# One-hots of the edge index from ScalarE to VectorE, and S1·T1 of row pairs in seven products of quarters, in a relational graph layer

## The chip, the cores and the metric

The kernel runs on one core of one Trainium2 chip. The metric is device time in microseconds (us) of one execution. The text calls the engines as the profile does: PE (TensorE, matmuls), PEld (its weight loads), DVE (VectorE), ACT (ScalarE), POOL (GpSimd), SP (SyncE, which issues DMAs).

## What is computed

1250 nodes have 1024 features each; 20,000 edges have a source, a target and one of 8 types. After a layer norm and a relu, h is multiplied with eight weight matrices of 1024 x 1024; every node takes, per type, the mean of its incoming neighbours' products, plus h times a root matrix; a gate with tanh mixes the result with h. In short:

```python
h = maximum(layernorm(x), 0)
u = h @ root + bias
for r in range(8):
    mask = edge_type == r
    sums = segment_sum(h[src] * mask, dst)
    cnt = segment_sum(mask, dst)
    u = u + (sums / maximum(cnt, 1)) @ weight[r]
z = concatenate([u, h]) @ w_gate + b_gate
out = x + tanh(u) * z + h * (1 - z)
```

All values are f32. The edges' sources, targets and types are inputs, so the order of the edges must be worked out on the chip.

## The kernel before

**Matrices and products.** The kernel multiplies h with each of the eight weights first and gathers rows of the products afterwards. There are eleven matrices in `mats`: the eight weights (numbers s = 0 to 7), the root, and two halves of the gate matrix. The text counts them from one: matrix two is s = 1. h stands in ten blocks of 128 rows, and product i (0 to 4) of a matrix takes blocks i and i + 5. Of these two blocks and the matrix it makes a 2 x 2 arrangement, A11, A12, A21, A22 times B11, B12, B21, B22, each B a quarter of 512 x 512, and forms the result by seven products in place of eight: A11·B11, A12·B21, S4·B22, A22·T4, S1·T1, S2·T2, S3·T3, where S and T are sums of A and B quarters (`left`, L406, and `make_t1` to `make_t4`, L172 to L186, on DVE). Every one of the seven is four f32 matmuls of 128x512 (`add`, L428, rows L430). The function `product` (L414) writes them out in a fixed order: p1 (A11), p5 (S1, L485), S2, p7 (S3), p3 (S4), A22. Results go from PSUM to a row tile by copies on ACT and by adds on DVE.

**Pairs.** In matrices two to ten, products 0 and 1, and 2 and 3, make a pair (`paired`, L571). The first of a pair is the head; the fifth product, number 4, stands alone (`lone`). Two products of a pair have the same B quarter in each of the seven, so such a quarter can again be cut 2 x 2, into pieces of 256 x 256, and formed by seven products of quarters, each two matmuls of 128x256 (`Second.add`, L219, rows L221). Class `Second` (L188) does this for A12·B21, class `First` (L323) for A11·B11 in all paired matrices, class `Third` (L261) for S4·B22 from matrix five on. `First` runs half of its work ahead, at the end of the product before (`early`, L343), and the rest in the head (`late`, L354): its two results lie in two PSUM banks, `to0` for the head and `to1` for the second product. Its sums are in a small room of SBUF tiles (`room`); `sums` and `next_sums` (L274, L280: two rows of 128x256 and two of 128x512 each) fill it twice. S1·T1 is done whole in both products of a pair, 4 matmuls in each (p5).

**PSUM.** There are eight banks: four named ps (`bank`, L122), two named ps_b (`lead`), one ps_n, one ps_q.

**Steps.** After each part, `done` (L434) calls `between` with a running number. `beside` (L618) hangs the matrix sums and weight loads on these numbers, and then one step of whatever else is to be done beside the products. From the first matrix to the fourth that is `norms_and_index` (L1368): a generator that goes one piece further at every step, except at the (product, step) places listed at L1385. `fill` places the quarter products between the parts.

**The index.** `slots` (L1080) goes over the edges in rounds of four chunks of 128. Each round takes two steps. In the first, `one_hots` (L1095) writes `is_lo` (which of 128 low key values an edge has, four tiles of 128x128 in bf16) by |a - b| (four ACT rows, L1100) and relu(1 - x) (one ACT row, L1102), and `is_at` on DVE (L1105). In the second, PE looks up and counts (`look` L1165, `count` L1111, bf16 matmuls), DVE takes the counts (`pick`, `add_counts`, `residue`), `place` (L1182) finds each edge's rank by four rows at L1190, and `to_los` (L1157) writes the other one-hot, 128x512, by two ACT rows (L1161, L1162). Counts of a round use the one-hots of the round before; the lookup of a round uses sums from the round before it. Every four rounds `to_table` (L1196) works out the places of up to 16 chunks, and `scatter` (L1067) issues two indirect DMAs of POOL at each step (rows L1071). `order` (L1220) and `rows_and_weights` (L809) follow; the rows are gathered (`add_slot`, L1422) beside matrices six and later.

**Queues.** Each engine works in program order. SP and ACT issue weight loads and plain stores, POOL the indirect DMAs.

Of the kernel before, what the change touches and what calls it, by code (L numbers as in the profile page):

```python
# [21 lines left out]
def tile_rgcn_highway(  # L22
# [31 lines left out]
    nc = tc.nc  # L54
# [28 lines left out]
    LATE = 4  # L83
    IDLE = 12
# [36 lines left out]

    def bank():  # L122
        return psum.tile([P, 512], F32, name="ps", bufs=4)

# [136 lines left out]
    class Third:  # L261
# [24 lines left out]
        def hold(self):  # L286
            self.c0 = psum.tile([P, CG, P], F32, name="ps_n", bufs=1).rearrange("p c k -> p (c k)")
            return self.c0
# [76 lines left out]

    def transposed(aop, part, of, n, relu=False):
# [47 lines left out]
    def product(aop, w, to, between=lambda j: None, last=None, pieces=1, whole=True,  # L414
                fill=None, second=None, third=None, inner=None, first=None, early=None, own=(),
                aside=None, head=False, lone=False):
# [21 lines left out]
        def filled(name):  # L438
            if fill and name in fill and fill[name]():
                done()  # L440

# [9 lines left out]
        def p7():  # L451
            d = c21 if third is None else aside()
            add(b, S3)
            nc.scalar.copy(d, b)  # L454
            nc.vector.tensor_add(c22, c if lone else c22, d)  # L455
            done()
            filled("seventh")
            return d
# [16 lines left out]
        def p1():  # L475
            if first is None:
                b = lead()
                add(b, A11, True)
            else:
                b = first.late() if head else first.to1  # L480
            nc.scalar.copy(c11, b)  # L481
            done()
# [3 lines left out]
        def p5(c=None):  # L486
            if c is None:
                c = inner.hold() if inner and inner.holds else held("ps_n")
# [9 lines left out]
        if first and head and early is None and "first" not in fill:  # L498
            c = inner.hold() if inner else bank()
# [15 lines left out]
        filled("sixth")  # L515
# [67 lines left out]
    waiting, waiting_third, waiting_first = {}, {}, {}  # L583
# [10 lines left out]
    def step(s, i, between=lambda j: None, second=None):  # L594

        two = paired(s, i)
        if (s, i) == (NM - 2, NP - 1):
# [5 lines left out]
        if two and i % 2 == 0:  # L603
            waiting[i] = Second(fac[s], i), t[0]

# [12 lines left out]
        def beside(j):  # L618
# [6 lines left out]
            if two and i % 2 == 0 and j == 3:  # L625
                waiting_first[s, i].fifth_to()
# [14 lines left out]
            if (s, i, j) == (0, 0, 3) or (s > 0 and (i, j) == (3, int(thirds(s)))):  # L641
# [27 lines left out]
        coming = next_first(s, i)  # L669

# [10 lines left out]
        if two:  # L681
# [18 lines left out]
            elif i == 1:  # L700
# [7 lines left out]
                else:  # L708
                    fill.update(seventh=lambda: (e.fourth(), e.to_second(t[0]),
                                                 put(i - 1, 0, to), 0)[-1],  # L710
                                third=lambda: (e.fourth_to_second(t[0]), 0)[-1])
            elif i == 2 and q:
# [9 lines left out]
            elif q:  # L722
                fill = dict(first=lambda: (q.first(t[1][:, :Q]), e.fourth(), e.to_second(t[0]),
# [4 lines left out]
            else:  # L728
                fill = dict(first=lambda: (e.to_second(t[0]), e.fourth_to_second(t[0]), 0)[-1],
# [4 lines left out]
                head=i % 2 == 0, lone=i == NP - 1,  # L734
# [9 lines left out]

    for _ in range(IDLE):
        nc.tensor.matmul(bank()[:, :P], ident, ident, start=True, stop=True)
    eps = const.tile([P, 1], F32, name="eps")
# [88 lines left out]
    with ExitStack() as early:  # L836
# [151 lines left out]
        less_lo = ix1.tile([P, NCH], F32, name="less_lo")  # L988
# [5 lines left out]
        less_pid = ix1.tile([P, 1], F32, name="less_pid")  # L994
# [6 lines left out]
        def columns():  # L1001
# [49 lines left out]
            nc.vector.tensor_single_scalar(less_lo, part_i, -1.0, op=OP.mult)  # L1051
# [8 lines left out]
            nc.vector.tensor_single_scalar(less_pid, pid, -1.0, op=OP.mult)  # L1060
# [6 lines left out]
        def scatter(count):  # L1067

            for c in placed[:count]:
                n = nedges(c)  # L1070
                ins = nc.gpsimd.indirect_dma_start(  # L1071
                    out=table[:, :],
                    out_offset=bass.IndirectOffsetOnAxis(ap=at_i[:n, c:c + 1], axis=0),
                    in_=row_col[:n, c:c + 1], in_offset=None,
                    bounds_check=G * KEYS * SLOTS - 1, oob_is_err=False)
                tc.declare_no_dep(ins.ins, query=no_wait, group="scatter", reason="each edge has its own slot")
                tc.add_to_no_dep_group("scatter", ins.ins)
            del placed[:count]

        def slots(ix):  # L1080
# [14 lines left out]
            def one_hots(j):  # L1095
# [3 lines left out]
                for i in range(m):  # L1099
                    nc.scalar.activation(is_lo[:, i, :], io, AF.Abs,  # L1100
                                         bias=less_lo[:, c0 + i:c0 + i + 1])
                nc.scalar.activation(is_lo[:, :m, :], is_lo[:, :m, :], AF.Relu, scale=-1.0,  # L1102
                                     bias=1.0)
# [53 lines left out]
            def to_los(j):  # L1157
# [3 lines left out]
                nc.scalar.activation(to_lo[:, :m, :], o["l_bc"][:, :m, :], AF.Abs, bias=less_pid)  # L1161
                nc.scalar.activation(to_lo[:, :m, :], to_lo[:, :m, :], AF.Relu, scale=-1.0,  # L1162
                                     bias=1.0)
# [32 lines left out]
            def to_table(c0, c1):  # L1196
# [3 lines left out]
                over = ix.tile([P, AT * CG], F32, name="over", bufs=1)  # L1200
                nc.vector.tensor_single_scalar(over[:, :m], rank[:, at], float(SLOTS), op=OP.is_ge)
                where = ix.tile([P, AT * CG], F32, name="where", bufs=1)
                nc.vector.tensor_add(where[:, :m], first[:, at], rank[:, at])
                nc.vector.scalar_tensor_tensor(at_i[:, at], over[:, :m], float(FAR), where[:, :m],  # L1204
                                               op0=OP.mult, op1=OP.add)
                placed.extend(range(c0, c1))

            load_keys(0)
            for j in range(ng + 3):
                for f, of in ((one_hots, j), (load_keys, j + 1), (as_bf16, j - 2),  # L1210
# [3 lines left out]
                    if f is None:  # L1214
                        scatter(CG // 2)
# [4 lines left out]
        def order():  # L1220

            with tc.tile_pool(name="sort", bufs=1) as sp:
# [12 lines left out]
                for _ in range(7):  # L1235
# [661 lines left out]
```

## Time and profile before

| what | value |
|---|---|
| median of 3 runs | 1334.18 us (1333.55 to 1334.95) |
| the profiled execution's own time | 1332.95 us |
| its span, first to last instruction | 1331.2 us |
| granted TensorE clock, mean | 0.998 |
| busy PE / DVE / ACT / POOL | 1318.1 / 957.4 / 386.8 / 573.4 us |
| L1100, L1102 on ACT | 157 rows, 50.1 us; 40 rows, 0.39 to 0.63 us each |
| L1161, L1162 on ACT (to_lo) | 39 rows of 128x512 each, 28.1 and 24.6 us |
| L1190 on DVE | 157 rows, 55.0 us, each with a read of its accumulator of 0.08 us |
| first and last start of L1071 (scatters) | 123.1 and 414.2 us |

A row of the profile groups instructions of one line, engine, operation and tile names: "out<-in" with their partitions and elements, how many, busy time together and the mean of one. Busy times of one engine count overlapping rows once. The views used below are the page, the waits, the timeline (instructions in order of time) and stretches (busy time of each engine in given windows).

### The profile page before, as it was taken

To read this page: it belongs to the slowest core of one execution; us is meant where nothing else is said; L and a number is where in the kernel's file an instruction comes from. 1 tells how busy PE (TensorE), PEld (TensorE's weight loads), DVE (VectorE), ACT (ScalarE), POOL (GpSimd) and SP (SyncE) were. 2 spreads that over 40 slices of the span, in tenths; PEclk is the share of its full clock that TensorE was granted. 3 is DMA by queue.
4 is the path that set the end of the run, shared out by engine and by line. 5 is a ranking of instruction groups with operands and counts; after the bars stand their busy time and mean duration, and the time that the engine had idled before them with its cause. 6 is when DMAs were issued, how large, how long until landed. Compare 5 with 4: busy or idle time off the path is not lost.

```text
span 1331.2 us, 13340 instructions
## 1 busy us (share of the span) xinstructions
PE 1318.1 (99%) x4120; PEld 716.5 (54%) x4120; DVE 957.4 (72%) x1825; ACT 386.8 (29%) x800; POOL 573.4 (43%) x510
## 2 busy tenths in 40 slices
PE   9999999999999999999999999999999999999997
PEld 5444555555455545655655565565565556644443
DVE  7757755665674664458987988897788799857875
ACT  3476556464621111211121211122121112221210
POOL 0002663744553156202353546446255556615631
PEclk9999999999999999999999999999999999999999
DMA  8877346642734251143748779877778957969961
GB/s 315 295 222 198 63 92 139 139 77 69 185 75 96 87 114 47 52 158 122 251 127 315 240 249 351 280 245 270 264 265 317 350 184 244 318 247 295 343 166 60
DMA packets 116799, 263.72 MB, mean 198 GB/s; under 512 B 33150, under 2 KB 44818, under 8 KB 116592
## 3 DMA queue, kind: packets, MB, share of 16 engines
q1 hardware_dynamic: 56528, 112.62, 28.1%
q0 software_dynamic: 44064, 118.20, 28.0%
q10 hardware_dynamic: 16128, 31.98, 7.8%
q8 instruction: 33, 0.54, 0.2%
q14 instruction: 46, 0.38, 0.1%
HBM read 202.34 MB, written 75.41 MB: 209 GB/s over the span
## 4 chain that ended last, share of the span: by engine, by line
PE 91%; issue 3%; DMA 2%; DVE 2%; POOL 1%; SPq 1%; ACT 0%; POOLq 0%; DVEq 0%
PE ps_b L430 44%; PE ps L430 18%; PE ps L221 14%; PE ps_n L430 5%; PE ps_b L221 4%; PE ps_q L221 2%; PE ps_q L430 2%; PE ps_n L221 2%; DMA xt<-in_x_dram 1%; DMA w<-in_L_gnn_weight_dram 1%; DMA h_op<-in_L_gnn_b_gate_dram 0%; POOL out_dram L770 0%; SPq L850 0%; PE ps L373 0%; PE ps_q L1114 0%
## 5 line engine op out<-in xcount | busy, mean ns | idle before, releaser
L430 PE MATMUL ps_b<-w,h_op 128*128 128x512 f32 x1464 | 659.7, 595 | 1.0 <-ACT row L513 0.8
L430 PEld LDWEIGHTS ps_b<-w,h_op 128*128 128x128 f32 x1464 | 273.6, 190 | 308.1 <-issue 296.4
L1425 POOL DMA_INDIRECT got<-y,idx x193 | 247.6, 1283 | 289.8 <-DVE u L1430 183.3
L1430 DVE SCALAR_TENSOR_TENSOR u<-got,w_of,u 128x1024 f32<-128x1024 f32 (+1 forms) x193 | 247.0, 1282 | 36.3 <-DMA got<-y,idx 33.2
L430 PE MATMUL ps<-w,h_op 128*128 128x512 f32 (+1 forms) x592 | 264.9, 589 | 0.3 <-ACT row L493 0.3
L1071 POOL DMA_INDIRECT table<-row_col,at_i x157 | 168.6, 1074 | 135.4 <-DVE at_i L1204 52.1
L430 PEld LDWEIGHTS ps<-w,h_op 128*128 128x128 f32 x592 | 111.0, 190 | 121.4 <-issue 115.0
L454 ACT COPY row<-ps_b 128x512 f32<-128x512 f32 x53 | 31.1, 586 | 188.0 <-PE ps_b L430 188.0
L455 DVE TENSOR_TENSOR row<-row 128x512 f32<-128x512 f32 x44 | 30.3, 689 | 75.2 <-ACT row L454 75.2
L430 PE MATMUL ps_n<-w,h_op 128*128 128x512 f32 x176 | 80.1, 592 | 0.0
L513 ACT COPY row<-ps_b 128x512 f32<-128x512 f32 x54 | 31.6, 586 | 162.1 <-PE ps_b L430 162.1
L221 PE MATMUL ps<-w,h_op 128*128 128x256 f32 x288 | 74.4, 381 | 0.0
L221 PE MATMUL ps<-w,w 128*128 128x256 f32 x288 | 71.1, 380 | 0.0
L553 ACT COPY row<-ps_b 128x512 f32<-128x512 f32 x40 | 23.4, 585 | 161.1 <-PE ps_b L430 140.8
L221 PEld LDWEIGHTS ps<-w,h_op 128*128 128x128 f32 x288 | 54.1, 190 | 27.6 <-issue 21.6
L221 PE MATMUL ps<-inner 128*128 128x256 f32 x264 | 67.8, 379 | 0.0
L221 PEld LDWEIGHTS ps<-w,w 128*128 128x128 f32 x288 | 54.6, 190 | 21.8 <-issue 15.8
L1190 DVE SCALAR_TENSOR_TENSOR junk<-k_bc,key_col,before 128x128 f32<-128x128 int16 x157 | 55.0, 350 | 4.2
L221 PEld LDWEIGHTS ps<-inner 128*128 128x128 f32 x264 | 50.1, 190 | 14.6 <-issue 8.4
L430 PEld LDWEIGHTS ps_n<-w,h_op 128*128 128x128 f32 x176 | 33.4, 190 | 39.5 <-issue 39.2
L481 ACT COPY row<-ps_b 128x512 f32<-128x512 f32 x54 | 31.6, 586 | 73.3 <-PE ps_b L430 68.7
L1100 ACT ACTIVATE is_lo<-io,less_lo 128x128 bf16<-128x128 f32 x157 | 50.1, 391 | 0.0
(246 smaller groups left out, 1473.7 us busy)
## 6 DMA issues: line engine op xcount, KB each, us to landing
y<-row SPq DMA_DIRECT2D x72, 512.0 KB
w<-in_L_gnn_weight_dram ACTq DMA_DIRECT2D x21, 1024.0 KB
w<-in_L_gnn_weight_dram SPq DMA_DIRECT2D x10, 1024.0 KB
w<-in_L_gnn_w_gate_dram ACTq DMA_DIRECT2D x6, 1024.0 KB
k_bc<-keys_dram SPq DMA_DIRECT2D x39, 128.0 KB
l_bc<-los_dram SPq DMA_DIRECT2D x39, 128.0 KB
h_dram<-h_op SPq DMA_DIRECT2D x9, 512.0 KB
u<-in_L_gnn_bias_dram SPq DMA_DIRECT2D x9, 512.0 KB
```

Of the source, the lines that this page charges most:

```text
L221: nc.tensor.matmul(p, a[:, k, :], b[:, k, :], start=(fresh and k == 0), stop=(k == 1), skip_group_check=True)
L430: nc.tensor.matmul(b[:, at], aop[:, i, k, :], w.of[i][:, k, at], start=(fresh and k == 0), stop=(k == KQ - 1), skip_group_check=True)
L454: nc.scalar.copy(d, b)
L455: nc.vector.tensor_add(c22, c if lone else c22, d)
L481: nc.scalar.copy(c11, b)
L513: nc.scalar.copy(c12, b)
L553: nc.scalar.copy(c21, b)
L1071: ins = nc.gpsimd.indirect_dma_start(out=table[:, :], out_offset=bass.IndirectOffsetOnAxis(ap=at_i[:n, c:c + 1], axis=0), in_=row_col[:n, ...
L1100: nc.scalar.activation(is_lo[:, i, :], io, AF.Abs, bias=less_lo[:, c0 + i:c0 + i + 1])
L1190: nc.vector.scalar_tensor_tensor(junk, o["k_bc"][:, i, :], key_col[:, c:c + 1], before, op0=OP.is_equal, op1=OP.mult, accum_out=rank[:, c: ...
L1425: nc.gpsimd.indirect_dma_start(out=t[:n], out_offset=None, in_=y[g][:, :], in_offset=bass.IndirectOffsetOnAxis(ap=at[:n, d, k:k + 1], axis=0),
L1430: nc.vector.scalar_tensor_tensor(u[:n], t[:n], w, u[:n], op0=OP.mult, op1=OP.add)
```

## The change

There are two parts, and some that go with them.

S1·T1 of the pairs of matrices two to five (`FIFTHS`, s from 1 to 4) is formed by a new class `Fifth`, seven products of quarters. Its first result lies in bank ps_n, its second in a kept bank of the four ps, set up once by a matmul on the identity. In the head it begins before A11, adds a quarter after it, does two after S2 and three after S3; the second product has no S1·T1 matmuls of its own. A step with the number 9 (`TICK`) is added after S3 of a head, and one after S2 of product 2; two places, (1, 1) and (3, 1), join the list at L1385. The quarter products of A12 move to other places of products 2 and 3. The lone product of these matrices uses the kept bank for S1·T1. Of the 12 matmuls on the identity at the start, four become one of 512 columns.

The one-hots `is_lo` and `to_lo` are written by DVE in one compare each: `is_lo` from a bf16 copy of the counting row against a column of low key values, `to_lo` from the int16 keys against the partition's number. The positions of a round are made at the start of the next steps, four chunks at a time, and the round's four scatters are issued there.

```diff
+    def sum_bank(odd):
+        if odd:
+            if not kept:
+                kept.append(bank())
+                nc.tensor.matmul(kept[0].rearrange("p (c k) -> p c k", c=CG), ident,
+                                 ident[:, None, :].to_broadcast([P, CG, P]), start=True, stop=True)
+            return kept[0]
+        return psum.tile([P, CG, P], F32, name="ps_n", bufs=1).rearrange("p c k -> p (c k)")
...
+    class Fifth:
...
+        def begin(self):
+            self.to0 = sum_bank(0)
+            self.x = bank()[:, :H]
+            Second.add(self, self.x, self.a11, self.b11, True)
+            nc.scalar.copy(self.to0[:, :H], self.x)
+        def second(self):
+            Second.add(self, self.to0[:, :H], self.a12, self.b21)
+        def early(self):
+            y = bank()[:, :H]
+            Second.add(self, y, self.s1, self.t1, True)
+            nc.scalar.copy(self.p5, y)
+            Second.add(self, self.x, self.s2, self.t2)
+            nc.vector.tensor_add(self.to0[:, H:], self.x, self.p5)
+        def late(self):
+            self.to1 = sum_bank(1)
+            Second.add(self, self.x, self.s1, self.t1)
+            nc.scalar.copy(self.to1.rearrange("p (a n) -> p a n", a=2),
+                           self.x[:, None, :].to_broadcast([P, 2, H]))
+            Second.add(self, self.to0[:, H:], self.s2, self.b22)
+            Second.add(self, self.to1[:, :H], self.a22, self.t2)
+        def fifth_to(self):
+            nc.vector.tensor_add(self.to1[:, H:], self.to1[:, H:], self.p5)
...
     def p7():
             add(b, S3)
             nc.scalar.copy(d, b)
+            if root and head:
+                between(TICK)
+                root.late()
+                nc.scalar.copy(c22, c)
+                root.fifth_to()
...
     def p1():
                 b = first.late() if head else first.to1
+            if root and head:
+                root.sums()
+                first.fifth_to()
             nc.scalar.copy(c11, b)
+            if root and head:
+                root.second()
...
     def p5(c=None):
+            if root:
+                c = root.to1
...
+        if root and head:
+            root.begin()
+            c = root.to0
+            if inner:
+                inner.c0 = c
+            b = p1()
...
         nc.scalar.copy(c12, b)
         done()
-        filled("sixth")
+        if root and head:
+            root.early()
+            root.next_sums()
+        if not filled("sixth") and root and head:
+            done()
...
                 for i in range(m):
-                    nc.scalar.activation(is_lo[:, i, :], io, AF.Abs,
-                                         bias=less_lo[:, c0 + i:c0 + i + 1])
-                nc.scalar.activation(is_lo[:, :m, :], is_lo[:, :m, :], AF.Relu, scale=-1.0,
-                                     bias=1.0)
+                    nc.vector.tensor_scalar(is_lo[:, i, :], io_b, lo_col[:, c0 + i:c0 + i + 1],
+                                            None, op0=OP.is_equal)
...
-                nc.scalar.activation(to_lo[:, :m, :], o["l_bc"][:, :m, :], AF.Abs, bias=less_pid)
-                nc.scalar.activation(to_lo[:, :m, :], to_lo[:, :m, :], AF.Relu, scale=-1.0,
-                                     bias=1.0)
+                nc.vector.tensor_scalar(to_lo[:, :m, :], o["l_bc"][:, :m, :], pid, None,
+                                        op0=OP.is_equal)
...
-                if s > 0 and (i, j) in ((0, 0), (1, 5), (NP - 1, 4)):
+                if s > 0 and (i, j) in ((0, 0), (1, 1), (1, 5), (3, 1), (NP - 1, 4)):
```

## The prediction

> **What bounds the kernel now.** I read four views, from the whole to the place. First the page: its head, its busy times, the row PE and the granted clock in the 40 slices, and the chain that ended last.
>
> ```profile
> span 1331.2 us, 13340 instructions
> ...
> PE 1318.1 (99%) x4120; PEld 716.5 (54%) x4120; DVE 957.4 (72%) x1825; ACT 386.8 (29%) x800; POOL 573.4 (43%) x510
> ...
> PE   9999999999999999999999999999999999999997
> ...
> PEclk9999999999999999999999999999999999999999
> ...
> PE 91%; issue 3%; DMA 2%; DVE 2%; POOL 1%; SPq 1%; ACT 0%; POOLq 0%; DVEq 0%
> ```
>
> PE has work 99% of the span, at full clock, and the chain runs through it for 91%. So a matmul that is taken out shortens the run by its own length, as long as no new wait stands in its place. The waits of PE say how little other engines hold it up today: the longest that belongs to the products is one of 0.6 us.
>
> ```profile
> PE ps_b L430 <- ACT row L513: 0.8, 1, 0.8
> ...
> PE ps_b L221 <- ACT ps_b L347: 0.6, 1, 0.6
> ```
>
> Busy times of PE rows overlap, so I price a matmul by the timeline, from start to start (columns: start, length, engine, line):
>
> ```profile
> 406.16 3.60 PE L430 MATMUL ps<-w,h_op 128*128 128x512 f32 x8
> 409.59 1.89 PE L221 MATMUL ps<-w,w 128*128 128x256 f32 x8
> 411.32 3.60 PE L430 MATMUL ps_b<-w,h_op 128*128 128x512 f32 x8
> ```
>
> Eight records 512 wide take 409.59 - 406.16 = 3.43 us, eight 256 wide take 411.32 - 409.59 = 1.73: 0.429 and 0.216 a record. Each f32 matmul of the program leaves two records.
>
> Last, what the engines carry beside PE, matrix by matrix (columns: stretch, its length, busy us of PE, PEld, DVE, ACT, POOL):
>
> ```profile
> 128.00:250.00 122.00, 121.45 (x455) 65.00 (x455) 76.95 (x299) 70.45 (x174) 71.01 (x67) 1.00 0.56 110
> 250.00:372.00 122.00, 122.00 (x457) 65.44 (x456) 75.66 (x288) 69.16 (x170) 67.85 (x65) 1.00 0.48 110
> 372.00:490.00 118.00, 118.00 (x340) 62.41 (x339) 70.68 (x134) 20.20 (x42) 40.44 (x37) 1.00 0.43 93
> 490.00:607.00 117.00, 117.00 (x358) 66.99 (x357) 60.06 (x124) 20.84 (x42) 37.24 (x34) 1.00 0.26 84
> ```
>
> These are matrices two to five. In the first two of them the index work runs beside the products: DVE has 45 us to spare out of 122, ACT 52.
>
> **The change, part by part.**
>
> *The products.* In a pair, S1·T1 is now eight matmuls of 512 columns, 16 records: 16 x 0.429 = 6.87 us. Seven products of quarters are 14 matmuls of 256, 28 records: 28 x 0.216 = 6.05. That is 0.82 less per pair, and with four matrices of two pairs, **6.57 us off PE**. The order of instructions confirms the count: 64 matmuls of 512 go, 112 of 256 come, and two 512 wide ones on the identity are new. One of these replaces four 128 wide in the idle start, where PE then waits 1.2 us for L888 anyhow: 0. The other stands inside the second matrix, ahead of the first use of the kept bank: **+0.86**.
>
> *ACT.* A round loses four L1100, one L1102, L1161 and L1162: 4 x 0.39 + 0.63 + 0.72 + 0.63 = 3.54 us; 16 rounds a matrix, so ACT drops from 70 to about 14, plus three new copies a pair (0.36, 0.37, 0.57: the rows of L347, L349, L357). The 0.6 us at L347 comes while ACT still has one-hots queued before that copy; with them gone I take **-0.6**. Cover lost: none.
>
> *DVE.* A pair adds two sets of four sums and two adds: 2 x (0.42 + 0.69 + 0.42 + 0.69) + 2 x 0.43 = 5.3 us; rows on DVE start some 0.08 before the last one ends, so the queue pays 4.5. A round adds four compares against a column (128x128, bf16). No row has this form; bounds are 0.17 (16 wide, L1203) and 0.42 (256 wide, L275). I take L1059, the same operation on f32, 0.28, and 0.20 in the queue. The compare 512 wide is between 0.42 and 0.69 (256 and 512 wide sums); I take 0.54 (L888, 512 wide with columns as scalars), 0.46 in the queue. The writing of positions per round instead of per four adds about 0.08. So 4 x 0.20 + 0.46 + 0.08 = 1.34 a round, 21 a matrix. Matrix two: 77 + 21 + 9 = 107 of 121 us, 89%; matrices four and five have next to no rounds and come to about 80 and 69. [...]
>
> *Where DVE meets PE.* Before, the two halves of S1·T1 needed no sums, now the quarters wait for them twice in a head product. The tightest place is product 0 of matrix three (index work still on, no identity matmul). Zero is the start of its first quarter. PE: first quarter 0.86, three of the existing late quarters to 3.46, a12·b21 to 4.32, S2 to 7.75, counts 0.3, two quarters to 9.8, a quarter of A12 to 10.6, S3 to 14.1, counts 0.3: the late quarters start at **14.4**. DVE: L447 of the product before 0.2 to 0.8, T3 (L182, 2.3) to 3.0, a round's one-hots to 4.05, four sums to 6.0, add 6.3, sum 6.9, T4 (L186) to 9.1, sum 9.7, second half of the round (0.8 + four L1190 at 0.39 + 0.46) to 12.5, add 12.9, then S1' and T1' ready at **13.8**, S2' and T2' at 14.75 for 15.2 and 16.1. So 0.5 us is left. Product 2 has no T3 and T4 in the way and keeps over 1 us. What is queued behind on DVE is the end of that round and product 0's adds: at the last counts of the product DVE is some 3 us behind and PE about 0.25 early. I charge **+0.5** for both such matrices.
>
> *Small waits.* Each new late half has a copy of one bank by ACT in front of an accumulation into it; the same shape at L357 costs 0.06 to 0.10 today (1.09 against 1.03 in the timeline rows of L221): 8 x 0.08 = 0.6. In product 1 the long S1·T1 no longer covers the copies of the first quarters of A12: end of A22 to copied is two copies and an add-on cast, about 2.0 us, against 0.3 + 1.72 of PE: 0.1 to 0.2, four times, 0.5. The S4 product behind the copy of the held bank (0.59 + 0.2 against 0.86): 0 to 0.1, 0.3 in all. Together **+1.4** (0 to 3).
>
> *POOL and SP.* Scatters go out four a round instead of two a step, the same 157; the last one starts at 414, the table is first read at 489 (L764): 75 us of cover, cost 0. The first load of the next matrix moves one step, behind 0.86 us of PE, and is needed 20 us later: 0. [...]
>
> **Sum:** -6.57 + 0.86 - 0.6 + 0.5 + 1.4 = **-4.4 us**. Against the profiled execution that is 1332.95 - 4.4 = 1328.5; the median of the three timed runs is 1.2 above that execution, so the median should go from 1334.18 to about **1329.8**. About 0.2%, 2.7 us, is what a measurement of this kernel can tell from no change.
>
> **Rivals.**
>
> 1. *The gain arrives whole.* The small waits hide, as most ACT waits do on this page: -6.57 + 0.86 - 0.6 = -6.3, 1327.9. For it: PE rows show almost no gaps. Against: each of these copies sits between two matmuls on one bank.
> 2. *DVE's lag eats most of it.* DVE at 89% in matrices two and three catches up less often; PE waits about 0.5 us in some heads and at every second round's counts (32 rounds, 16 x 0.2 = 3.2): 1333. Against: L1177 today sits idle 32 us for PE's counts, so DVE has breaks to catch up in.
> 3. *DVE becomes the bound, slower.* One mechanism: counts of a round need the sums that DVE wrote a round before, so when DVE needs more time per matrix than PE (121), PE follows it. At 107 of work this happens once more than 14 us of DVE's 45 us of idle per matrix cannot be filled because it waits for PE there. With 20 unfillable, 6 us a matrix, 12 in two, less the 4.4: about +7, 1342. The idle in front of L1177, 31 us for both, is 16 a matrix: near that point, which is why I keep it.
> 4. *It does not do what it says* (quarters slower than 0.216, as S1·T1 goes through a bank that ACT fills first): 28 records would need 0.245 to lose the gain. All rows of L221 have 0.38 to 0.40 a record, those into banks that ACT filled (L357) too: below 2 in 100, counted with rival 2.
>
> **How the numbers follow.** Forecast 0.56 (-5.7 to -2.9); rival 1 0.16 (to -7); rival 2 0.18 (-2.9 to +2.7, most of it within 2.7); rival 3 0.10. Faster by over 0.2%: 0.56 + 0.16 and the 0.02 of rival 2 beyond the bound, 0.74; within: 0.16; slower: 0.10. The range goes from 1327.4, where the small waits and the lag cost nothing, to 1333.6, most of rival 2; rival 3 and the edges are left out, 0.18.
>
> **What would show it.** In the changed profile: L221's counterpart has 224 records more and the 512 wide ones 124 fewer; no is_lo row on ACT, DVE near 105 of 121 us in matrices two and three, ACT under 20; the gap at L347 near 129.8 gone. Waits of PE on DVE sums of the new class in product 0 of matrices two and three under 0.5 us each: forecast; on the counts' s_b at many rounds: rivals 2 and 3. A compare row well over 0.4 us, or PE below 98% anywhere in slices 4 to 11, would prove me wrong.

## The result and the profile after

The changed kernel takes **1331.38 us** (median of 16 runs, 1330.42 to 1334.63) against 1333.67 us for the kernel before (median of 16 runs): a ratio of 0.9984, 95% interval 0.9977 to 0.9990. One run of the kernel before, of 8048 us, is left out of the ratio; without it the median is 1333.55. So 2.2 to 2.3 us are gained where 4.4 were forecast, 1331.4 where 1329.8 was forecast. The profiled execution took 1331.68 us, 1.27 less than the profiled one of before.

First the page after: head, busy times, the row of PE and the chain that ended last.

```profile
span 1329.9 us, 13668 instructions
...
PE 1315.0 (99%) x4212; PEld 734.2 (55%) x4212; DVE 1028.2 (77%) x2132; ACT 279.5 (21%) x547; POOL 579.2 (44%) x510
...
PE   9999999999999999999999999999999999999997
...
PE 81%; issue 6%; DMA 5%; DVE 5%; POOL 2%; SPq 1%; ACT 1%; POOLq 0%; DVEq 0%
```

PE has 92 records more: 224 more of 256 columns, 124 fewer of 512, and 8 fewer of the 128 wide ones on the identity. ACT lost 107 us. PE still works 99% of the span. Its share of the chain fell from 91 to 81%: the chain now leaves PE for a stretch around 860 to 950 us, at a wait of half a microsecond that is told below. Then the waits of PE (engine, tile and line that waited, for what; total, times, longest):

```profile
PE ps L235 <- ACT w L252: 1.0, 3, 0.5
...
PE ps L491 <- ACT row L569: 0.8, 2, 0.5
...
PE ps L235 <- ACT w L241: 0.5, 1, 0.5
PE ps L235 <- DVE inner L290: 0.3, 1, 0.3
```

L235 is the quarter product (L221 before), L491 the whole one (L430). The wait of L221 for ACT's copy L347 is gone. Three new kinds stand there, two of them for copies by ACT, L252 and L241; and the wait for c22's copy (L569, L493 before) was 0.3 us once and is now 0.8, twice. And the stretches of matrices two to five (stretch, length, busy us of PE, PEld, DVE, ACT, POOL):

```profile
128.00:250.00 122.00, 121.74 (x484) 70.42 (x483) 98.92 (x401) 25.50 (x67) 66.42 (x65) 1.00 0.54 111
250.00:371.00 121.00, 120.25 (x472) 69.31 (x471) 98.00 (x395) 24.17 (x63) 69.80 (x62) 1.00 0.55 107
371.00:488.00 117.00, 116.54 (x371) 66.46 (x370) 77.92 (x170) 22.27 (x47) 47.43 (x40) 1.00 0.37 96
488.00:605.00 117.00, 117.00 (x387) 72.52 (x386) 73.79 (x150) 23.81 (x49) 40.40 (x37) 1.00 0.30 85
```

DVE is at 99 of 122 us in matrix two (107 were forecast), ACT at 25. PE is no longer busy through the second and third stretch: 0.75 and 0.46 us are missing.

**Where the time went.** From start to start, a PE record of 512 columns takes 0.429 us and one of 256 takes 0.216. What lies beyond that between two starts is a gap; its sum over the run tells what PE waited, also where the waits above count less. In the names, c11 to c22 are the four quarters of a product's result; e.first to e.seventh are the quarter products of A12·B21 of a pair. L241 copies e.first's result out of the bank to which e.sixth adds, L252 that of e.seventh out of the bank to which e.fourth adds.

| stage (us from the start) | gaps before | gaps after | what is new |
|---|---|---|---|
| 0 to 8.7, first transposes | 3.70 | 4.29 | x's DMA lands 0.65 later |
| 8.7 to 125, matrix one | 1.99 | 2.59 | 0.62 at 71.4, c22's copy (L569) |
| 125 to 250, matrix two | 2.44 | 2.21 | L347's 0.65 gone; 0.40 at 216.5, L252 |
| 250 to 371, matrix three | 1.54 | 3.05 | 0.64 at 287.9 (L241), 0.41 at 338.4 (L252), 0.17 (L419) |
| 371 to 605, matrices four, five | 1.14 | 2.02 | 0.62 at 456.4 (L252) |
| 605 to the end | 4.86 | 5.44 | 0.51 at 952.4 (L290) |

By their numbers, PE's records became 6.57 - 0.86 = 5.71 us shorter, as forecast; the gaps grew by 3.9; the last matmul starts 1.7 earlier, and 0.45 of that is lost behind it, where the last rows are stored.

**The theories.** *A*: the gain is real and whole on PE, and what ate it are copies by ACT that stand between two matmuls on one bank: with S1·T1 gone from the second product of a pair, too little PE work is left to cover them. *C*, the rival (rival 2 of the prediction): DVE's load of 99 of 122 us makes PE wait for sums and counts. *B* stands in single runs for "a wait taken away only moves".

The wait for L241 at 287.9, which the view of the waits puts down to ACT, goes back to DVE:

```profile
286.77 0.59 ACT L552 COPY row<-ps_b 128x512 f32<-128x512 f32 x1
286.82 0.75 DVE L1212 TENSOR_SCALAR is_lo<-io_b,lo_col 128x128 bf16<-128x128 bf16 x4
...
287.20 1.03 PE L235 MATMUL ps<-w,w 128*128 128x256 f32 x4
...
287.87 0.22 DVE L1232 TENSOR_TENSOR seen<-seen,ps_q 128x80 f32<-128x80 f32 x1
...
288.13 0.26 ACT L1257 CAST s_b<-seen 128x80 bf16<-128x80 f32 x1 [0.76 <-DVE seen L1232]
288.29 0.36 ACT L241 COPY w<-ps 128x256 f32<-128x256 f32 x1
```

ACT is done with c11's copy (L552) at 287.36 and then idles 0.76 us in front of the cast of the counts, which needs DVE's row L1232; L241 stands behind the cast. DVE comes late to that row, with the round's four compares in front of it. In matrix two the same four ACT rows follow each other without a break, from 165.47 to 167.00, and PE has no gap there. onehots_again has the compares on DVE too, but a whole S1·T1 behind e.first, and no gap there: so this wait takes both parts of the change. It is theory C by way of ACT's queue. no_setup and after_again show the same idle time of ACT, 0.76 and 0.77 us.

### The profile page after: what moved, and what is told of

The parts are those of the page before. It is cut to its first block, busy times and chain, and to the rows that moved or that the text cites. A ratio compares the mean times of both kernels' runs of the same rounds, so it can differ in the third digit from the quotient of the medians.

```text
span 1329.9 us, 13668 instructions
## 1 busy us (share of the span) xinstructions
PE 1315.0 (99%) x4212; PEld 734.2 (55%) x4212; DVE 1028.2 (77%) x2132; ACT 279.5 (21%) x547; POOL 579.2 (44%) x510
## 4 chain that ended last, share of the span: by engine, by line
PE 81%; issue 6%; DMA 5%; DVE 5%; POOL 2%; SPq 1%; ACT 1%; POOLq 0%; DVEq 0%
PE ps_b L491 39%; PE ps L235 16%; PE ps L491 11%; PE ps_n L491 5%; PE ps_b L235 3%; PE ps_n L235 2%; DMA got<-y,idx 2%; PE ps_q L235 2%; PE ps_q L491 2%; DMA xt<-in_x_dram 1%; POOL got L1533 1%; DMA w<-in_L_gnn_weight_dram 1%; DVE u L1538 1%; POOL out_dram L878 0%; DVE h_op L472 0%
## 5 line engine op out<-in xcount | busy, mean ns | idle before, releaser
L491 PE MATMUL ps_b<-w,h_op 128*128 128x512 f32 x1464 | 659.1, 594 | 1.0 <-ACT row L595 0.8
L491 PEld LDWEIGHTS ps_b<-w,h_op 128*128 128x128 f32 x1464 | 274.4, 190 | 305.0 <-issue 294.2
L1184 POOL DMA_INDIRECT table<-row_col,at_i x157 | 172.6, 1099 | 154.6 <-DVE at_i L1180 109.0
L491 PE MATMUL ps<-w,h_op 128*128 128x512 f32 (+1 forms) x432 | 192.1, 586 | 0.8 <-ACT row L569 0.8
L491 PEld LDWEIGHTS ps<-w,h_op 128*128 128x128 f32 x432 | 81.1, 190 | 91.5 <-issue 85.9
L491 PE MATMUL ps_n<-w,h_op 128*128 128x512 f32 x208 | 94.4, 593 | 0.0
L235 PE MATMUL ps<-inner 128*128 128x256 f32 x360 | 91.6, 380 | 0.3 <-DVE inner L290 0.3
L235 PE MATMUL ps<-w,h_op 128*128 128x256 f32 x320 | 83.0, 382 | 1.0 <-ACT w L252 1.0
L235 PEld LDWEIGHTS ps<-inner 128*128 128x128 f32 x360 | 67.8, 190 | 18.6 <-issue 9.0
L235 PEld LDWEIGHTS ps<-w,h_op 128*128 128x128 f32 x320 | 59.9, 190 | 28.8 <-issue 20.2
L595 ACT COPY row<-ps_b 128x512 f32<-128x512 f32 x54 | 31.6, 585 | 205.1 <-PE ps_b L491 205.1
L235 PE MATMUL ps<-w,w 128*128 128x256 f32 x288 | 70.8, 380 | 0.5 <-ACT w L241 0.5
L235 PEld LDWEIGHTS ps<-w,w 128*128 128x128 f32 x288 | 54.3, 190 | 20.1 <-issue 13.4
L491 PEld LDWEIGHTS ps_n<-w,h_op 128*128 128x128 f32 x208 | 39.3, 190 | 45.1 <-issue 44.2
L552 ACT COPY row<-ps_b 128x512 f32<-128x512 f32 x54 | 31.7, 587 | 83.5 <-PE ps_b L491 76.1
```

The costliest lines, as they stand in the source:

```text
L235: nc.tensor.matmul(p, a[:, k, :], b[:, k, :], start=(fresh and k == 0), stop=(k == 1), skip_group_check=True)
L491: nc.tensor.matmul(b[:, at], aop[:, i, k, :], w.of[i][:, k, at], start=(fresh and k == 0), stop=(k == KQ - 1), skip_group_check=True)
L595: nc.scalar.copy(c12, b)
L1184: ins = nc.gpsimd.indirect_dma_start(out=table[:, :], out_offset=bass.IndirectOffsetOnAxis(ap=at_i[:n, c:c + 1], axis=0), in_=row_col[:n, ...
```

## The experiments

Ratios are to the kernel before, run beside it on the same chip. These runs came from three chips. On one of them (runs fourth_later, no_setup, all_three, onehots_again) the kernel before took 1333.5 us, as above. On the two others it took 1383.6 and 1380.3, and the profiles from there show PE stalls of 2 to 5 us in matrices two to four (2.6, 3.2 and 4.3 in after_again, 4.8 in more_dve) that those of the first chip, but for fourth_later's waits for a load, don't show. Times from different chips are therefore not compared; from the slower chips I read single waits that stand at the same place with the same length in two profiles, and ratios of kernels that ran side by side.

**after_again**: the changed kernel, unedited.

> The changed kernel once more, for a second profile of the same program. Theory A (the gain is smaller than forecast because PE waits for ACT's copies out of a bank that its next matmul adds to): ratio to before about 0.9984, and the three waits of PE for the copy L252, about 0.4, 0.4 and 0.6 us near 216, 338 and 456 us, and the one for L241 of 0.6 near 288 stand in this profile too. Theory B (these gaps are chance of one execution): they are gone or elsewhere. The later start of the first transposes (0.65 us), the gap of 0.6 at 71 and that of 0.5 at 952 lie outside the changed products: under both theories I expect at least two of the three not to come again.

Measured: 0.9744 (0.9722 to 0.9766), 1347.9 us. The waits came again at their places: L252 0.40, 0.81 and 0.63 us, L241 0.65, c22's copy at 71 us 0.66. They belong to the program. The first L491 starts 0.65 us earlier, as in before, and there is no gap at 952; these two vary between executions, so two of the three other gaps went, as expected. The third, in matrix one, stays and belongs to the change. The ratio is another than on the first chip; see the last section.

**onehots_only** and **onehots_again**: one kernel, the one-hots alone, with the new order of the scatters.

```diff
-    FIFTHS = (1, 4)
+    FIFTHS = (1, 0)
...
-                if s > 0 and (i, j) in ((0, 0), (1, 1), (1, 5), (3, 1), (NP - 1, 4)):
+                if s > 0 and (i, j) in ((0, 0), (1, 5), (NP - 1, 4)):
...
-    for _ in range(IDLE - CG):
+    for _ in range(IDLE):
```

(and no identity matmul into ps_n at the start).

> The kernel before with only the one-hots on DVE and the positions a round at a time; no quarters for S1T1, the start and the list of skipped steps as before. Theory A: ACT's one-hots only delayed one copy, so the time falls by the 0.6 us of the gap at L347, 0.3 to 0.9: ratio about 0.9995. Theory C (DVE with some 20 us more a matrix makes PE wait for the counts or sums): ratio 1.000 to 1.003, with new waits of PE on DVE rows in matrices two to four.

> The kernel before with only the one-hots on DVE and the positions a round at a time, once more. Theory A: 0.3 to 0.9 us below before where PE has no long stalls (ratio 0.9993 to 0.9998); on a chip where before stalls for some 50 us, as in the last runs (1383.6 against 1333.7), again most of that is gone (ratio near 0.975). Theory C (DVE's load costs): above before where there are no long stalls.

Measured on the slower chip: 0.9751 (0.9725 to 0.9777). On the first chip, in the second run: **1.0006** (0.9997 to 1.0015), 1334.5 us: no gain where 0.3 to 0.9 us were expected. The gap at L347 is gone, but 0.80 us stand at 71 us in matrix one and 1.11 at 955. The timeline of matrix one shows why, first before, then with the one-hots on DVE (start, length, engine, line):

```profile
69.30 1.24 ACT L895 ACTIVATE h_op<-xt,less,rs 128x1024 f32<-128x1024 f32 x1 [0.42 <-DVE less L879]
...
70.45 0.56 ACT L493 COPY row<-ps 128x512 f32<-128x512 f32 x1
...
71.19 0.59 PE L430 MATMUL ps<-w,h_op 128*128 128x512 f32 x1
```

```profile
70.09 0.73 DVE L1210 TENSOR_SCALAR is_lo<-io_b,lo_col 128x128 bf16<-128x128 bf16 x4
70.21 1.24 ACT L1001 ACTIVATE h_op<-xt,less,rs 128x1024 f32<-128x1024 f32 x1 [0.42 <-DVE less L985]
...
71.35 0.57 ACT L569 COPY row<-ps 128x512 f32<-128x512 f32 x1
...
71.97 0.70 PE L491 MATMUL ps<-w,h_op 128*128 128x512 f32 x1 [0.63 <-ACT row L569]
```

In matrix one the layer norm still runs: DVE works out a row's statistics, ACT scales the row (1.24 us), and c22's copy queues behind it. The compares of the first round stand on DVE at 62.5 us, 0.63 us of its queue ahead of that chain; the chain ends 0.9 us later, and so does the copy that PE needs. Beyond that and the wait at 955, theory C found nothing on the first chip: DVE is at 92 of 122 in matrix two, and PE waits nowhere for counts.

On the first chip this also splits the change, roughly, as the intervals are some 0.1% wide to each side: the one-hots cost 0.06% (some 0.8 us), where -0.6 us was forecast, and the quarters bring 0.9984 / 1.0006, 0.22% or 2.9 us, where -6.57 + 0.86 + 0.5 + 1.4 = -3.8 was forecast.

**fifths_act** and **fifths_act_again**: the changed kernel with the ACT rows of before.

```diff
-                    nc.vector.tensor_scalar(is_lo[:, i, :], io_b, lo_col[:, c0 + i:c0 + i + 1],
-                                            None, op0=OP.is_equal)
+                    nc.scalar.activation(is_lo[:, i, :], io, AF.Abs,
+                                         bias=lo_col[:, c0 + i:c0 + i + 1])
+                nc.scalar.activation(is_lo[:, :m, :], is_lo[:, :m, :], AF.Relu, scale=-1.0,
+                                     bias=1.0)
```

(lo_col negated, to_lo in the same way).

> The changed kernel with the one-hots back on ACT; the quarters of S1T1 and the positions a round at a time stay. Theory A: the copies between two matmuls on one bank now queue behind ACT rows of 0.4 to 0.7 us each, four or five in a row, so PE waits 0.5 to 1.5 us at several of the new copies in matrices two and three: 3 to 8 us above the changed kernel, 1334.5 to 1339, no gain or a loss against before. Theory C (DVE is what limits): taking 20 us a matrix off DVE brings time, 1 to 3 us below the changed kernel.

> The changed kernel with the one-hots back on ACT, once more. Theory A (the new copies would queue behind ACT's one-hots): 3 to 8 us above the changed kernel, ratio 1.0005 to 1.004, with waits of PE for L419, L252, L241 and L361 of 0.5 to 2.7 us each. Theory C (DVE is the tight engine): at or below the changed kernel, ratio at most 0.9985.

Measured, both times on slower chips: 0.9846 (0.9822 to 0.9870), with after_again's 0.9744 beside it on the same chip, 13.3 us above it and so more than the 3 to 8 expected; and 0.9877 (0.9849 to 0.9905). A part of the 13.3 is the clock of the last section: in the stretches 128 to 250, 250 to 371 and 371 to 488 us it is 0.97, 0.97 and 0.99 in this profile, 0.99, 1.00 and 0.97 in after_again's, which comes, as an estimate from these means, to some 17 and 9 us at half clock. The waits of PE in the second profile:

```profile
PE ps L235 <- ACT w L252: 3.2, 3, 1.9
PE ps L235 <- ACT ps L419: 3.0, 2, 1.5
```

L252 went from 1.0 to 3.2 us, and L419, the copy that fills both halves of Fifth's kept bank, from next to nothing to 3.0; in the first profile the same two read 3.2 and 3.0, in after_again's 1.4 and none. Theory A: with ACT's one-hots in front of the copies, the quarters cost PE more waiting. How much of the 13 us would remain on the first chip wasn't measured.

**more_dve** and **more_dve_again**: each narrow compare twice.

```diff
-                    nc.vector.tensor_scalar(is_lo[:, i, :], io_b, lo_col[:, c0 + i:c0 + i + 1],
-                                            None, op0=OP.is_equal)
+                    for _ in range(2):
+                        nc.vector.tensor_scalar(is_lo[:, i, :], io_b,
+                                                lo_col[:, c0 + i:c0 + i + 1],
+                                                None, op0=OP.is_equal)
```

> The changed kernel with each of the 157 narrow compares made twice into the same tile: about 157 x 0.2 = 31 us more on DVE, some 11 a matrix in matrices two to four. Theory A (DVE has slack): within 0.7 us of the changed kernel, ratio to before 0.998 to 0.999. Theory C (DVE near its bound, its lag ate the gain): 3 to 7 us above the changed kernel.

> The changed kernel with each of the 157 narrow compares made twice, once more: 157 x 0.18 = 28 us more on DVE, about 10 in each of matrices two and three, so some 109 of 121 us busy there, close to what was forecast for the change itself. Theory A (DVE has slack): within 0.7 us of the changed kernel, ratio 0.998 to 0.999, where PE has no long stalls. Theory C (DVE's lag is what ate the gain, and grows): 3 to 7 us above the changed kernel, with PE waiting for DVE's sums and s_b in matrices two to four.

Measured on slower chips: 0.9867 (0.9842 to 0.9892), 17.2 us above after_again beside it, and 0.9861 (0.9835 to 0.9888). Matrix two of the first run, and a wait of the second:

```profile
128.00:250.00 122.00, 117.30 (x468) 68.33 (x467) 112.28 (x446) 24.77 (x63) 62.86 (x63) 0.99 0.50 98
```

```profile
PE ps_q L1280 <- DVE s_b L1266: 3.5, 1, 3.5
```

DVE is at 112 of 122 us, and here PE does wait for it: 3.5 us for s_b at the lookup near 168 us, 1.07 near 157 for the sums of S1·T1 (L296), in both profiles alike. Ahead of the first, DVE's rows follow each other without a break from 154 to 172. So theory A's claim that DVE has slack for 28 us more is wrong. None of these direct waits is in the changed kernel's profile; what DVE costs there are the two indirect ones, through ACT, at 71 and 287.9 us. The slack in front of the lookups ends between 99 and 112 us of 122. How much of the 17.2 us are stalls of this chip stays open.

**no_setup**: the kept bank is taken one product earlier.

```diff
-        narrow[0] = fifths(s)
+        narrow[0] = fifths(s) or (i == NP - 1 and fifths(s + 1))
...
-                nc.tensor.matmul(kept[0].rearrange("p (c k) -> p c k", c=CG), ident,
-                                 ident[:, None, :].to_broadcast([P, CG, P]), start=True, stop=True)
```

> The changed kernel without the identity matmul that sets up the kept bank inside matrix two: the kept bank is taken one product earlier, as the bank of S1T1 of the last product of matrix one, which writes it in full. Theory A (the two records of 512 columns stand on PE's path): 0.86 us below the changed kernel, ratio to before about 0.9978. Theory B (a wait behind it takes their place): unchanged, with a longer wait of PE near 155 us.

Measured: **0.9972** (0.9962 to 0.9983), 1329.9 us, the shortest time of all versions. Where the two records stood (154.45 to 155.39 us), the next quarter now follows the counts at once, with no wait in their place. Against the changed kernel's 0.9984 that is 1.6 us, with intervals that allow the 0.86 expected (theory A). Its profiled execution, 1331.9, was its slowest of eight and has 1.4 us of wait at 952.

**fourth_later** (the first hunk of fourth_later2's diff below) and **all_three** (with it no_setup's diff and the first two hunks of best's).

> The changed kernel, with the last product of quarters of A12 of the pair's second product (e.fourth, products 2 and 3 of matrices two to four) moved from the front of product 3 to behind S2, so that 3.4 us of PE stand between the copy L252 out of its bank and the next matmul into that bank. Theory A (the three waits for L252, 0.40 + 0.40 + 0.62 = 1.4 us, are part of what ate the gain): 1.4 us below the changed kernel, ratio to before about 0.9973, and no row of PE waiting for L252. Theory B (PE would have met another wait there, for c22's or c11's copy or for a free bank): within 0.4 us of the changed kernel, with a new wait in its place.

> The changed kernel with e.fourth behind S2 in product 3, without the identity matmul, and with the chain of A12's quarters in product 1 one part later as well (e.sixth behind S2, e.seventh behind S3, e.fourth behind S4), which takes the copy L241 out of PE's way (0.64 us once). Theory A: 1.4 + 0.86 + 0.6 = 2.9 us below the changed kernel, ratio to before about 0.9962. Theory B (waits are only moved): less than 1 us below, with new waits of PE on ACT's copies or on banks. Theory D (fewer free banks in product 1 make the early part of the next pair's A11 wait): above the changed kernel.

The edit put e.fourth behind S2 in product 3; that is also behind the load of the next matrix's first quarter, which goes into the tile that holds e.fourth's T4, and of the second, into the tile with p5 and p7. So both kernels form these parts with the next matrix's values, and all_three also leaves out e.seventh and its adds in product 1 of matrix five. Measured: 1.0134 (1.0119 to 1.0150) and 1.0116 (1.0100 to 1.0131). PE waits for the load:

```profile
221.47 0.26 PE L1223 MATMUL ps_q<-is_at,is_lo 128*128 128x80 bf16 x4
226.36 3.78 PE L235 MATMUL ps<-w,h_op 128*128 128x256 f32 x8 [4.63 <-DMA w<-in_L_gnn_weight_dram]
```

Their times say nothing on A or B, but they price a wait of PE (last section).

**fourth_later2**: the same with both loads one part later.

```diff
-                fill = dict(first=lambda: (root and e.fourth(), e.to_second(t[0]),
-                                           e.fourth_to_second(t[0]), 0)[-1],
-                            sixth=lambda: (e.second(), True),
+                fill = dict(sixth=lambda: (e.fourth(), e.to_second(t[0]),
+                                           e.fourth_to_second(t[0]), e.second(), True),
...
-            if (s, i, j) == (0, 0, 3) or (s > 0 and (i, j) == (3, int(thirds(s) or fifths(s)))):
+            if (s, i, j) == (0, 0, 3) or (s > 0 and (i, j) == (3, 1 if thirds(s) else 3 * fifths(s))):
...
-            if (s, i, j) == (0, 0, 3) or (s > 0 and (i, j) == (3, 2)):
+            if (s, i, j) == (0, 0, 3) or (s > 0 and (i, j) == (3, 3 if fifths(s) and not thirds(s) else 2)):
```

> The changed kernel with e.fourth behind S2 in product 3 of matrices two to four, and now also the two loads of the next matrix that overwrite its operands one part later, behind it. Theory A (the three waits for the copy L252, 1.4 us in all, are part of what ate the gain): 1.4 us below the changed kernel, ratio to before about 0.9973, no wait of PE for L252. Theory B (another wait takes their place: c11's or c21's copy in front of S2's matmuls, 0.9 to 1.1 us in the kernel before this one, stands there whether or not e.fourth is moved, as S2 adds to the bank that L552 copies): within 0.5 us of the changed kernel, with three waits for L552 in place of those for L252.

Measured on a slower chip: 0.9833 (0.9801 to 0.9865). PE's waits:

```profile
PE ps_b L491 <- ACT row L552: 3.0, 3, 1.3
```

No wait for L252 is left; three for L552 stand there, gaps of 0.89, 1.45 and 1.11 us where there were 0.40, 0.41 and 0.62 (0.89, 1.04 and 1.11 in fourth_later, on the first chip). Theory B: the wait moved and grew. The end of product 2 in the changed kernel shows why:

```profile
215.46 1.03 PE L235 MATMUL ps<-w,w 128*128 128x256 f32 x4
215.66 0.58 ACT L639 COPY row<-ps_b 128x512 f32<-128x512 f32 x1 [3.92 <-PE ps_b L491]
216.14 0.26 ACT L1257 CAST s_b<-seen 128x80 bf16<-128x80 f32 x1
...
216.42 0.26 PE L1224 MATMUL ps_q<-is_at,is_lo 128*128 128x80 bf16 x4
216.52 0.37 ACT L252 COPY w<-ps 128x256 f32<-128x256 f32 x1
...
216.79 0.59 ACT L552 COPY row<-ps_b 128x512 f32<-128x512 f32 x1
216.94 1.13 PE L235 MATMUL ps<-w,h_op 128*128 128x256 f32 x4 [0.26 <-ACT w L252]
```

ACT copies c21, casts counts, copies e.seventh's result (L252) and then c11, from 215.66 to 217.4. L252 doesn't wait for that queue: it starts 0.03 us after e.seventh's last matmul ends, at 215.46 + 1.03 = 216.49, and in matrices three and four ACT idles 0.53 and 0.28 us for that matmul. Its 0.37 us are then uncovered, but for the counts' 0.2; in matrix four, where no counts stand between, the gap is 0.62. c11's copy is queued behind L252 and ends 1.9 us after e.seventh's start. With e.fourth in its place PE has 0.86 + 0.2 + 0.36 + 0.97 = 2.4 us until S2, without it 1.1, and so waits 0.8 or more. Before, e.fourth stood behind A22, 3.43 us after e.seventh, and in product 3 a whole S1·T1, again 3.43, lay over c11's copy. c11's copy ahead of L252 in the queue was not tried.

**best**: fourth_later2, no_setup, A12's chain in product 1 one part later, and the first two rounds of is_lo on ACT (it too leaves out e.seventh and its adds in product 1 of matrix five, some 0.86 us of PE).

```diff
-                            fifth=lambda: (e.sixth(), True),
-                            sixth=lambda: (e.seventh(), e.to_first(to), 0)[-1])
+                            fifth=lambda: (root or e.sixth(), True),
+                            sixth=lambda: (e.sixth() if root else (e.seventh(), e.to_first(to)), 0)[-1])
...
-                    fill.update(seventh=lambda: (e.fourth(), e.to_second(t[0]),
-                                                 put(i - 1, 0, to), 0)[-1],
-                                third=lambda: (e.fourth_to_second(t[0]), 0)[-1])
+                    fill.update(seventh=lambda: (e.seventh(), e.to_first(to), 0)[-1],
+                                third=lambda: (e.fourth(), e.to_second(t[0]), put(i - 1, 0, to),
+                                               e.fourth_to_second(t[0]), 0)[-1])
...
+                    if j < 2:
+                        nc.scalar.activation(is_lo[:, i, :], io, AF.Abs,
+                                             bias=less_lo[:, c0 + i:c0 + i + 1])
```

> fourth_later2 with three more edits: no identity matmul in matrix two, A12's quarters of product 1 one part later each, and the first two rounds of is_lo on ACT again. Theory A: -0.86 for the identity, -0.64 for the wait on L241 in product 1, -0.6 for the wait at 71 us in matrix one (the norm's chain no longer behind the compares on DVE), and -1.4 or, by theory B of the run beside it, 0: 1.5 to 3.5 us below the changed kernel, ratio to before 0.9958 to 0.9973. If the waits only move, it is within 1 us of the run without the identity alone (0.9972).

Measured on the slower chip: 0.9799 (0.9766 to 0.9831), 4.9 us below fourth_later2 beside it, with intervals that overlap; 0.86 is the work left out, and stalls of that chip stand in both. By its profile the gap at 71 us is gone (c22's copy starts at 70.94, and PE goes on at 71.56 without a gap), and so is L241's near 300; the three for L552 (0.89, 1.43, 1.11) remain. A wait of 1.9 us for the copy behind e.sixth near 176 stands where this chip also stalls in other kernels and can't be put down to the edit. So, by this profile, the waits of matrix one and of L241 can be removed; that at the end of product 2 was only moved. What this is worth on the first chip wasn't measured.

## Why the forecast was right in kind and too large in size

The time lies in the range, but the gain of 2.2 to 2.3 us is smaller than the 2.7 us (0.2%) that it would exceed, by the prediction, with a chance of 0.74, and it lies outside the -5.7 to -2.9 of the forecast. By its size it falls to rival 2, whose mechanism, DVE's lag, is a part of what came.

*The products*: right. 224 records of 256 columns more, 124 of 512 fewer; 5.71 us net with the identity matmul, and quarters one behind the other keep 0.216 (rival 4 out). *The identity matmul* stands on the path, 0.94 us from its start to the next in the timeline, and no wait takes its place in no_setup.

*ACT, "-0.6. Cover lost: none"*: **this step failed, in its second half**. The gap at L347 went (0.65), but the one-hots that left ACT stand on DVE in matrix one, ahead of the norm's statistics, a stage that the prediction left out, as it priced the one-hots in matrices two to five alone. 0.6 to 0.9 us at 71 us in every profile with the compares on DVE there, none in before, fifths_act and best. The one-hots alone gave +0.06% in place of -0.05%.

*Small waits, "0.1 to 0.2, four times, 0.5"*: **mis-sized by four**. It priced product 1's e.sixth alone, for a queue of copies that in matrices two and four costs nothing. In its place: one wait of 0.64 there in matrix three (L241), as a cast in that queue waits for DVE, and 0.40, 0.41 and 0.62 in front of e.fourth in product 3 (L252), whose new place next to e.seventh got no term: 2.07 us. The other two small terms (0.6 and 0.3) are about what is left: matrices two to five gained 2.16 us of gaps net, 2.8 without L347's 0.65, and 2.8 less 2.07 is 0.7.

*DVE*: priced too high, and the lag of 0.5 us at product 0 didn't come; a wait of 0.64 came at product 1 instead, through ACT, so that the term's size is luck. In matrix two the one-hots cost 92.1 - 77.0 = 15 us (21 forecast) and Fifth's sums 98.9 - 92.1 = 7 (9 forecast). Four compares take 0.73 us on the queue, 0.16 from one to the next, not 0.20, and a single narrow one 0.25 (median), not 0.28; to_lo 0.36, not 0.54. The scatters' rows on POOL kept their length beside the compares: 1074 ns on average before, 1099 after, and 980 to 1120 each near 162 to 173 us in more_dve, with twice the compares.

*ACT's load*: "under 20" a matrix was forecast, 24 to 25 us came. The sum of 3.54 us a round added lengths of rows that overlap (four L1100 take 1.28 us in the timeline, not 4 x 0.39 = 1.56), which the prediction allowed for on DVE and not on ACT.

*Rivals 2 and 3*: PE waits for no count and no sum of the new class in this profile, but DVE's compares cost 0.62 us at 71 and 0.64 at 287.9, 1.3 of the 3.9 us by which the gaps grew; that much of rival 2 is real. At 112 us instead of 99, PE waits 3.5 us at a lookup. What a load of 107, as forecast, would have cost wasn't run; that direct waits stayed away owes something to the load being lower than forecast, and that is luck.

The sum with the measured terms: -5.71 - 0.65 + 2.8 (matrices two to five) + 0.6 (matrix one) = -3.0, against -2.3 in the medians and -1.3 in the profiled pair, which also has 0.6 at the start, 0.5 at 952 and 0.45 behind the last matmul. The wait at 952 is one of DVE, which waits for a gathered row: 0.5, 1.1 and 1.4 us in the profiles of the changed kernel, onehots_again and no_setup, none in before, and 0 to 1.1 where PE comes 13 to 30 us later. Whether the change brings it oftener, or only the phase of the gathers does, stays open, and so does what the new order of the scatters is worth by itself.

## What to carry to other kernels

When a long matmul is taken out of a chain, list the copies that ran beneath it, all of them and in the order of their queue, with what each of them waits for, and set the end of each against what is left of PE's work there: here 1.9 us to the end of c11's copy against 1.1 of quarters and counts. A copy behind a row that waits for a third engine takes on that engine's lag, here 0.76 us of ACT in front of L241. When work is moved to another engine, price it in every stage in which it runs, also in the one with few rounds, since what counts is whose chain it is put ahead of. And a waiting matmul that was moved behind the next one here only changed the copy that PE waited for, as the queue of copies stayed the same.

## What the runs showed of the hardware

*The value of this change depends on the chip.* On two chips the kernel before took 1383.6 and 1380.3 us, and on the first of these the changed one 0.9744 of that; onehots_only has nearly all of it (0.9751), and fifths_act, with the one-hots on ACT, a good half (0.9846). Both have the new order of the scatters, so the runs don't tell what the one-hots do there by themselves. In onehots_again (first chip) and onehots_only (slower chip), one program, PE's records start within 0.3 us of each other up to 165 us, yet ACT's copy L241 of a bank that PE filled starts 1.9 us later on the slower chip. First chip, then slower one:

```profile
162.04 0.59 ACT L552 COPY row<-ps_b 128x512 f32<-128x512 f32 x1
162.56 0.37 ACT L241 COPY w<-ps 128x256 f32<-128x256 f32 x1
```

```profile
161.78 0.59 ACT L552 COPY row<-ps_b 128x512 f32<-128x512 f32 x1
164.48 0.37 ACT L241 COPY w<-ps 128x256 f32<-128x256 f32 x1 [2.11 <-PE ps L235]
```

Such delays of 2 to 5 us between PE and the engines that wait for it come several times between 160 and 440 us, the stage of the index and its scatters, with waits of PE of 2.6, 3.2 and 4.3 us at 170.34, 179.31 and 423.89 in after_again; mostly they stand at the same places of a program on both slower chips (PE's longest waits for L595 and L241 are 4.8 and 3.1 us in more_dve, 5.5 and 3.1 in more_dve_again). The rows themselves take as long on both, 0.59 and 0.37 us here. The cause stays open; no run here takes it apart.

*A long wait of PE can cost more than its length.* In fourth_later, after 4.63 us of wait, eight records of 256 take 229.94 - 226.36 = 3.58 us instead of 1.73, and the granted clock is 0.50 from 224.6 to 231.4:

```profile
224.60:231.40 6.80, 5.04 (x10) 3.54 (x11) 0.00 (x0) 0.00 (x0) 0.81 (x1) 0.50 0.69 238
```

In after_again the granted clock is 0.99 from 128 to 250 us and 0.97 from 371 to 488. Behind its wait of 3.2 us three records of 512 take 2.61 us, where three at 173.45 take 1.45; behind that of 4.3 us four records of 256 take 2.08, where four at 416.82 take 1.03; behind that of 2.6 us four take 1.13, where four at 164.89 take 1.11. What decides whether a wait has this effect, these runs don't show. The waits of 0.4 to 0.6 us in the changed kernel show no such effect: its mean clock is 0.998, as before.
